# Other order for the second image's direct products around the logits' turns, and a second form for the third image's row at infinity

## The chip, the cores and the metric

The kernel runs on one core of a Trainium2 chip. The metric is the device time of one execution in microseconds (us). Before the change the median of three runs is 669.0 us (668.98, 669.0, 670.58).

The core has five engines that run side by side and wait for each other by semaphores: PE (matrix products; PEld is its loading of weights), DVE (elementwise work), ACT (copies, activations), POOL (here mostly issues of transfers and clearing of buffers) and SP (here only issues of transfers). Each works through its own list of instructions in order.

## The reference

Four images of 256 channels and 64x64 pixels. A 7x7 convolution with dilation 2 and a 1x1 convolution give 49 logits per pixel. Their softmax weights the 49 shifted copies of the image (local attention). The result is whitened in groups of 64 channels.

```python
k = lax.conv_general_dilated(x, w1, (1, 1), [(6, 6), (6, 6)], rhs_dilation=(2, 2), ...) + b1
k = lax.conv_general_dilated(k, w2, (1, 1), [(0, 0), (0, 0)], ...) + b2
attn = softmax(k, axis=1)
xp = jnp.pad(x, ((0, 0), (0, 0), (6, 6), (6, 6)))
shifts = jnp.stack([xp[:, :, 2*u:2*u+64, 2*v:2*v+64] for u in range(7) for v in range(7)], axis=1)
x = jnp.einsum('bkchw,bkhw->bchw', shifts, attn)
# then: mean and 64x64 covariance of each group over all pixels, five Newton steps for
# the inverse square root, and its product with the centred x
```

## The kernel before, in words

The weights of both convolutions are folded into one 7x7 convolution from 256 channels to 49 logits. Everything is float32; the trace records two matmuls for each that the kernel names. Pixels are split by the parity of their row: slot tiles (`slot2`, `slot3` for image 1) each hold one parity of an image.

**The convolution** is done by a Winograd-like scheme: rows are evaluated at seven points, columns at seven points, the products are taken point by point, and both directions are interpolated. Points in a row direction are numbered `br`: 1 to 5, 0, and 6, "infinity" (`INF`). For br 1 to 5 there are products with evaluated data (`conv_bank`, PE at L604, in three banks of column points). The columns are then interpolated into `zz[:, br]` (`col_interp`), and the rows into the logits (`row_interp`, in two parts).

For some rows the columns are not evaluated; the products run directly over the seven column taps:
- `direct` (L779) takes 7 taps x 2 channel chunks x 2 parities (x 2 halves of the columns), 56 matmuls for a whole row at infinity of a later image. So it is done for the row at infinity of images 2 and 3 (`direct_inf`).
- `direct_part` (L862) does the same in three products, each over half as many columns: part 2 takes the even taps, part 1 the odd taps, part 3 the sums of two neighbouring taps with sums of two neighbouring columns of x. Part 3 minus the others gives the odd columns (`direct_ends`). `direct_sums` makes the sums, on DVE. So it is done for image 1's row at infinity and for image 1's row 0 (`direct_start`).

Banks of PSUM: two `cv` banks that are taken in turn (`conv_psum`, `conv_bank`), and two `acc` banks, later used for the attention's sums `y`.

**After the logits** of an image come, for each of two column parities, its turn: PE transposes the logits (L1135), DVE takes the maximum, ACT the exponentials with sums, DVE reciprocals, products and four shuffles (`soft`, `softmax`). Then ACT copies the terms into `zt` (L1253), POOL writes them to memory as `sd` (L1272), and SP reads them back in banded form into `band` and `bandz` (L1322, L1334). PE multiplies the transposed image with the bands (L1442, `first_half` and `second_half`) and turns the result back for the covariance (L1514, L1533).

**What sets the order.** Engines run their lists in order. The first image's part is emitted under `strict[0] = True`: each DVE operation made by `add`, `sub` or `madd` then stands behind the one before it. Later work is a list of steps with costs for each image; after each eighth of the image's cost comes a "gap", in which a half block of the attention of the image before is put (`todo`, `half_gaps`). `conv_step(k, i)` emits bank `i` of row `k` and then prepares the same bank of the next row at once, or, if a gap with a half block follows and the next row is a row 0 at its first bank (`half_next`), behind that gap.

**Around the change**, before: DVE evaluates the first bank of image 1's row 1 (`prepare(NR0, 0)`), then makes the sums for image 1's row at infinity (`direct_sums` into `gbr`, two adds of 512 columns and three of 98), then adds the second half of row 5 of image 0 to `zz` and goes through the second part of `row_interp(0, 1)`, which ends image 0's logits. PE does parts 2 and 1 of the row at infinity into `acc`, then part 3 into a `cv` bank. Then image 0's turn (`soft(0, 0)`), `direct_start(0)` (sums; parts 2 and 1 of row 0 into the two `cv` banks), `direct_start(1)` (part 3 into `acc[0]`), the other turn (`soft(0, 1)`), and the first `conv_step`.

Of the kernel before, what the change touches and what calls it, by code (L numbers as in the profile page):

```python
# [23 lines left out]
INF = 6  # L24
# [8 lines left out]
def kernel(  # L33
# [772 lines left out]
    def direct_sums(b, br, w, room):  # L806

        a = 3 if br == INF else 0
        xs = []
        for h in range(2):  # L810
            x = slots[2 * b + h].rearrange("p c r w -> p (c r w)").rearrange(
                "p (e a w) -> p a e w", a=4, w=SW
            )
            x = x[:, a].rearrange("p e (m i two) -> p i e m two", i=2, two=2)
            o = room[:, h * NX // 2 : (h + 1) * NX // 2]
            add(o.rearrange("p (e m two) -> p e m two", m=SW // 4, two=2), x[:, 0], x[:, 1])
            xs.append(
                o.rearrange("p (c g q w) -> p c g q w", c=NCC, g=2, q=Q8).rearrange(
                    "p c g q (m two) -> p c g q m two", two=2
                )  # L820
            )
        ws = []
        for s, t in enumerate(w):
            nw = (KS // 2) * NCC * KT
            o = room[:, NX + s * nw : NX + (s + 1) * nw]
            o = o.rearrange("p (v a k) -> p v a k", v=KS // 2, a=NCC)
            for j in range(KS // 2):
                add(o[:, j], t[2 * j + 1], t[2 * j])
            ws.append([o[:, j] for j in range(KS // 2)] + [t[KS - 1]])
        return xs, ws  # L830

    def direct_part(b, br, part, ps, w, xs=None):
# [10 lines left out]
        first = True  # L843
        for wt, d in order:
# [51 lines left out]

    def direct_inf(b):

        nc.sync.dma_start(spare[:, :NTAP], kept[INF])
        t = spare[:, :NTAP].rearrange("p (v a k) -> p v a k", v=KS, a=NCC)  # L900
        direct(b, INF, 0, conv_psum(), [t[:, v] for v in range(KS)])

    start_of = {}

    def direct_start(sr):

        n = Q8 + 1
        w = [[gr0[:, v, :, s] for s in range(2)] for v in range(KS)]
        if sr == 0:
            room = store[4].rearrange("p c r w -> p (c r w)")[:, SH * W :]  # L910
            xs, ws = direct_sums(1, 0, [[t[s] for t in w] for s in range(2)], room)
            start_of["xs"] = xs
            start_of["ws"] = [[t[j] for t in ws] for j in range(KS // 2 + 1)]
            p2 = direct_view(conv_psum(), n, M16 + 1)
            direct_part(1, 0, 2, p2, w)
            p1 = direct_view(conv_psum(), n, M16)
            direct_part(1, 0, 1, p1, w)
            direct_ends(0, n, p1, p2)
        else:
            p3 = direct_view(acc[0], n, M16)  # L920
# [3 lines left out]
    acc = [ps_y.tile([P, Q8, W], F32, tag="y", name=f"acc{sr}") for sr in range(2)]  # L924
    for a in acc:
        nc.vector.memset(a, 0.0)
# [14 lines left out]
    def conv_step(k, i):  # L941
# [13 lines left out]
        if k + 1 < len(rows):  # L955
            if half_next[0] and (i, rows[k + 1][1]) == (0, 0):
                after_gap.append(lambda: prepare(k + 1, i, points.append))
            else:
                with tc.high_priority() if last else nullcontext():
                    prepare(k + 1, i, points.append)  # L960
        if i == len(BANKS) - 1 and not end:
# [115 lines left out]
    w = [tap[:, UPOS[3], v] for v in range(KS)]  # L1077
    xs, ws = direct_sums(1, INF, [w], gbr.rearrange("p v a s k -> p (v a s k)"))
    direct0(5, 1)
    row_interp(0, 1)  # L1080

    w = [[t] for t in w]
    p2 = direct_view(acc[0], Q8, M16 + 1)
    direct_part(1, INF, 2, p2, w)
    p1 = direct_view(acc[1], Q8, M16)
    direct_part(1, INF, 1, p1, w)
    p3 = direct_view(conv_psum(), Q8, M16)
    direct_part(1, INF, 3, p3, [[t] for t in ws[0]], xs)
    prepare(NR0, 1)
    prepare(NR0, 2)  # L1090
    strict[0] = False
    direct_ends(INF, Q8, p1, p2)
    direct_ends(INF, Q8, None, None, p3)
# [612 lines left out]
    for b in range(1, B):  # L1706
# [6 lines left out]
        if b == 1:  # L1713
            for sr in range(2):
                steps.insert(sr, (12, lambda sr=sr: direct_start(sr)))
            steps.insert(0, (0, lambda: soft(0, 0)))
            steps.insert(3, (0, lambda: soft(0, 1)))
# [316 lines left out]
```

## Time and profile before

| | |
|---|---|
| median of three runs | 669.0 us |
| the profiled execution | 668.98 us |
| its span, first to last instruction | 667.2 us |
| mean granted PE clock | 0.991 |
| instructions | 19415 |
| DMA packets, bytes | 109840, 126.11 MB |

PE's records by stage of the kernel, from its instructions in order of time:

| stage | us |
|---|---|
| image 0, preparation and its products | 0 to 142.5 |
| image 1, row at infinity in three products | 142.5 to 153.3 |
| first turn of image 0's logits | 154.9 to 156.1 |
| image 1, row 0 in three products | 156.1 to 175.2 |
| image 1's other rows, with image 0's attention between | from 176.8 |
| image 2, row at infinity by `direct` | 273.0 to 284.6 |
| whitening (L1844) | from 613.0 |

How to read it: a line of the time order gives start, length, engine, line of the kernel, operation, output and inputs, size and count; in brackets stands the idle time of that engine before it and what ended it. Matmuls are pipelined, so a record of about 270 ns starts every 55 to 60 ns. "SPq" and "ACTq" are issues of transfers; the data land later. Idle time of an engine that others don't wait for costs nothing.

### The profile page before, as it was taken

What the parts mean: (1) busy time and instruction counts of PE and PEld (TensorE: products, weight loads), DVE (VectorE), ACT (ScalarE), POOL (GpSimd) and SP (SyncE); (2) the same over time, 40 slices, a digit from 0 to 9 for tenths busy, and PEclk for the clock granted to TensorE, in tenths of its full rate; (3) what the DMA queues carried; (4) which work ended last, traced back from release to release, by engine and by line L of the source; (5) the groups of instructions that cost most, each with busy time, mean ns of one, the idle gap of its engine ahead of it and who ended that gap; (6) DMA issues with size and microseconds to landing.
All of it is one profiled execution on the core that took longest, in us unless ns stands there. A gap on an engine that the chain in (4) does not pass through costs nothing.

```text
span 667.2 us, 19415 instructions
## 1 busy us (share of the span) xinstructions
PE 638.7 (96%) x7992; PEld 530.1 (79%) x7992; DVE 571.2 (86%) x1258; ACT 331.8 (50%) x861; POOL 115.3 (17%) x173
## 2 busy tenths in 40 slices
PE   6999999999999999999999999999999999999991
PEld 1439673358999998889999998999999999997440
DVE  3699999999899889999999799989999988634781
ACT  1434331013565566467754554473855667535681
POOL 0000551663213002001022020002220203500000
PEclk9999999999999999999999999999999999999996
DMA  8961799995599988324588673026364325739698
GB/s 316 247 177 67 128 232 382 218 195 83 133 205 223 228 257 304 103 57 108 149 278 278 232 246 107 1 69 195 103 197 112 70 65 129 182 96 380 263 412 335
DMA packets 109840, 126.11 MB, mean 189 GB/s; under 512 B 69127, under 2 KB 92216, under 8 KB 107576
## 3 DMA queue, kind: packets, MB, share of 16 engines
q1 hardware_dynamic: 92952, 69.35, 35.5%
q0 software_dynamic: 10752, 37.26, 21.7%
q10 hardware_dynamic: 6048, 18.27, 8.8%
q8 instruction: 63, 1.03, 0.7%
q14 instruction: 25, 0.20, 0.1%
HBM read 78.78 MB, written 52.36 MB: 197 GB/s over the span
## 4 chain that ended last, share of the span: by engine, by line
PE 62%; DVE 17%; issue 7%; POOL 4%; SPq 4%; DMA 3%; ACT 2%; DVEq 0%; ACTq 0%; POOLq 0%
PE cv L604 25%; PE y L1442 13%; PE sig L1533 5%; PE tp L1514 4%; PE tp L1378 4%; SPq L225 4%; POOL ahead L147 2%; POOL slot L147 2%; PE tp L1844 2%; PE cv L862 2%; DVE zz L352 2%; DVE rb L345 2%; PE cv L779 2%; DVE xh L352 2%; DVE pv L352 1%
## 5 line engine op out<-in xcount | busy, mean ns | idle before, releaser
L604 PE MATMUL cv<-xh,wr 128*49 128x128 f32 x4160 | 232.3, 273 | 0.1
L604 PEld LDWEIGHTS cv<-xh,wr 128*49 128x49 f32 x4160 | 226.2, 124 | 2.9 <-issue 1.0
L1272 POOL DMA_DIRECT2D sd<-zt x120 | 63.3, 534 | 292.2 <-ACT zt L1253 222.2
L1442 PE MATMUL y<-band,xb 128*128 128x209 f32 x448 | 93.7, 341 | 0.6 <-ACT xb L1409 0.6
L1442 PEld LDWEIGHTS y<-band,xb 128*128 128x128 f32 x448 | 75.7, 191 | 1.5 <-ACT xb L1409 0.8
L615 ACT COPY pv<-cv 113x486 f32<-113x486 f32 (+2 forms) x60 | 25.9, 431 | 82.4 <-PE cv L604 82.2
L352 DVE SCALAR_TENSOR_TENSOR pv<-pv 113x162 f32<-113x162 f32 x176 | 52.5, 320 | 1.5 <-ACT pv L615 1.0
L1524 ACT COPY yt<-tp 128x512 f32<-128x512 f32 x60 | 35.0, 591 | 24.3 <-PE tp L1514 23.5
L1253 ACT COPY zt<-d 32x112 f32<-32x112 f32 (+2 forms) x132 | 38.6, 293 | 11.0 <-DVE d L1123 5.1
L1514 PE MATMUL tp<-ident,slot 128*128 128x128 f32 x240 | 41.3, 295 | 0.2 <-ACT slot L1464 0.2
L1378 PE MATMUL tp<-ident,slot 128*128 128x128 f32 x256 | 40.5, 282 | 0.0
L1175 ACT ACTIVATE d<-tp,mx 128x49 f32<-128x49 f32 x96 | 27.4, 321 | 24.2 <-DVE mx L1172 17.6
L1533 PE MATMUL sig<-yt 128*64 128x65 f32 x1024 | 38.0, 225 | 0.9 <-ACT yt L1524 0.9
L1514 PEld LDWEIGHTS tp<-ident,slot 128*128 128x128 f32 x240 | 34.9, 205 | 5.0 <-issue 3.7
L1378 PEld LDWEIGHTS tp<-ident,slot 128*128 128x128 f32 x256 | 38.2, 204 | 0.2 <-issue 0.2
L1533 PEld LDWEIGHTS sig<-yt 128*64 128x64 f32 x1024 | 32.9, 137 | 6.7 <-issue 1.9
L1409 ACT COPY xb<-tp 128x512 f32<-128x512 f32 x52 | 30.6, 588 | 13.7 <-PE tp L1378 10.5
L352 DVE SCALAR_TENSOR_TENSOR xh<-ct 128x512 f32<-128x512 f32 x40 | 26.6, 691 | 5.7 <-PE cv L604 5.4
L147 POOL DMA_DIRECT2D slot<-in_x_dram x12 | 20.4, 1701 | 53.4 <-DVE xh L352 38.6
L348 DVE TENSOR_TENSOR pv<-pv 113x162 f32<-113x162 f32 (+1 forms) x77 | 27.5, 364 | 0.3
L352 DVE SCALAR_TENSOR_TENSOR xh<-xh,rb 128x512 f32<-128x512 f32 x40 | 27.4, 684 | 0.1
L345 DVE TENSOR_TENSOR ct<-rb 128x1024 f32<-128x1024 f32 (+1 forms) x26 | 26.5, 1020 | 0.3
(288 smaller groups left out, 1141.9 us busy)
## 6 DMA issues: line engine op xcount, KB each, us to landing
band<-sd SPq DMA_DIRECT2D x64, 242.0 KB, 3.6
sd<-zt POOLq DMA_DIRECT2D x120, 77.0 KB, 4.2
wr<-gd ACTq DMA_DIRECT2D x14, 588.0 KB, 4.8
wr<-gd ACTq DMA_DIRECT2D x14, 490.0 KB, 4.1
slot<-in_x_dram POOLq DMA_DIRECT2D x12, 512.0 KB, 10.5
ahead<-in_x_dram POOLq DMA_DIRECT2D x12, 512.0 KB, 7.8
spill<-slot POOLq DMA_DIRECT2D x3, 2048.0 KB, 9.4
slot<-ahead POOLq DMA_DIRECT2D x3, 2048.0 KB, 10.7
```

Source lines behind the costliest of these rows:

```text
L147: yield queue.dma_start(o[:, cc, h], src[:, :, pr, h * SW : (h + 1) * SW])
L345: return in_turn(TT(o, a, b, ALU.add))
L352: return in_turn(STT(o, a, f, b, ALU.mult, ALU.add))
L604: nc.tensor.matmul(o, wv[:, sc, sr, cc], xv[bc][:, h * NCC + cc], start=(j == 0), stop=(j == len(terms) - 1), skip_group_check=True,)
L1253: ins = nc.scalar.copy(o, i)
L1272: dma = queue.dma_start(bass.AP(tensor=D.tensor, offset=D.offset + h * HS + g * RS, ap=[[LS, TC], [CR * RS, NCH], [1, KS * WS]],), zt[p0 : ...
L1378: nc.tensor.transpose(t[:, h * C + cc * P : h * C + (cc + 1) * P], tile_of(xt, cc, t8, h, pc), turned_by(n),)
L1409: (nc.vector.tensor_copy if n > 4 * B - 3 else nc.scalar.copy)(xb.rearrange("p a c -> p (a c)"), t[:, : 2 * C])
L1442: nc.tensor.matmul(y_ps[n, half, cc][:, q0 : q0 + nq, c0:c1], xb[:, cc * P : (cc + 1) * P], rhs, start=(k == 0), stop=(k == len(PIECES[hal ...
L1514: nc.tensor.transpose(t[:, h * C + cc * P : h * C + (cc + 1) * P], tile_of(yt, cc, t8, h, pc), turned_by(n),)
L1524: return nc.scalar.copy(yb.rearrange("p h a g c -> p (h a g) c")[:, :, :GW], t[:, : 2 * C].rearrange("p (e c) -> p e c", c=GW),)
L1533: nc.tensor.matmul(sig[g * GW : (g + 1) * GW, cc], yb[:, g, :GW], yb[:, g], start=(count[0] == 0), stop=end, skip_group_check=True,)
```

## The change

Three things, as the code has them:
1. `direct_sums` takes the place for the sums of taps as an argument, and `direct_taps` makes them in one add over all pairs instead of three for each share.
2. Image 1's direct products stand in another order. Parts 2 and 1 of the row at infinity are emitted before `row_interp(0, 1)`, and their ends right behind it; its sums are made between `prepare(NR0, 1)` and `prepare(NR0, 2)`, no longer under the strict order, with x sums in `spare` (the third buffer of `pv`), tap sums in `lgx`, and the last tap copied there by ACT. Its part 3 goes to `third_inf`, into `acc[0]`, in the third step of `direct_start`. `direct_start` now has three steps: sums and the first two taps of part 2; the other two taps and part 1; `third_inf` and part 3, now in `acc[1]`. The turn `soft(0, 0)` stands between the first and the second.
3. `direct_inf` has a second form with three products, whose results are copied out of PSUM by ACT, for an image whose sums `inf_sums` has made ahead. `inf_sums` is called in `conv_step`, in the branch that prepares the next row at once.

```diff
@@ -803,7 +803,7 @@
-    def direct_sums(b, br, w, room):
+    def direct_sums(b, br, w, room, sums):
 
         a = 3 if br == INF else 0
         xs = []
@@ -819,17 +819,17 @@
                     "p c g q (m two) -> p c g q m two", two=2
                 )
             )
-        ws = []
-        for s, t in enumerate(w):
-            nw = (KS // 2) * NCC * KT
-            o = room[:, NX + s * nw : NX + (s + 1) * nw]
-            o = o.rearrange("p (v a k) -> p v a k", v=KS // 2, a=NCC)
-            for j in range(KS // 2):
-                add(o[:, j], t[2 * j + 1], t[2 * j])
-            ws.append([o[:, j] for j in range(KS // 2)] + [t[KS - 1]])
-        return xs, ws
-
-    def direct_part(b, br, part, ps, w, xs=None):
+        return xs, direct_taps(w, sums)
+
+    def direct_taps(w, sums):
+
+        n = w.shape[2]
+        o = sums[:, : KS // 2 * n].rearrange("p (v n) -> p v n", n=n)
+        pair = w[:, : KS - 1].rearrange("p (v two) n -> p two v n", two=2)
+        add(o, pair[:, 1], pair[:, 0])
+        return [o[:, j] for j in range(KS // 2)] + [w[:, KS - 1]]
+
+    def direct_part(b, br, part, ps, w, xs=None, some=slice(None)):
 
         a = 3 if br == INF else 0
         if part == 2:
@@ -840,8 +840,8 @@
             order = [(wj, j - 1) for j, wj in enumerate(w)]
         order.sort(key=lambda p: abs(p[1]))
         lo = -1 if part == 2 else 0
-        first = True
-        for wt, d in order:
+        first = not some.start
+        for wt, d in order[some]:
             for cc in range(NCC):
                 for s in range(len(wt)):
                     for g in range(2):
@@ -894,36 +894,90 @@
+    ahead_inf = {}
+
+    def inf_sums(b):
+
+        nc.sync.dma_start(spare[:, :NTAP], kept[INF])
+        room = rb[1].rearrange("p q r c w -> p (q r c w)")
+        t = spare[:, :NTAP].rearrange("p (v n) -> p v n", v=KS)
+        ahead_inf[b] = direct_sums(b, INF, t, room, room[:, NX:])
+
     def direct_inf(b):
 
+        if b in ahead_inf:
+            xs, ws = ahead_inf[b]
+            t = spare[:, :NTAP].rearrange("p (v a k) -> p v a k", v=KS, a=NCC)
+            one = lambda t: [t.rearrange("p (a k) -> p a k", a=NCC)]
+            w = [[t[:, v]] for v in range(KS)]
+            z = zz[:K2, INF, :Q8].rearrange("p q (m i two) -> p i q m two", i=2, two=2)
+            n2 = Q8 * (M16 + 1) * 2
+            room = rb[1].rearrange("p q r c w -> p (q r c w)")[:K2, 2 * NX - n2 :]
+            copy = direct_view(room.rearrange("p (q w) -> p q w", q=Q8), Q8, M16 + 1)
+            banks = [conv_psum() for _ in range(2)]
+            p3 = direct_view(banks[0], Q8, M16)
+            direct_part(b, INF, 3, p3, [one(t) for t in ws], xs)
+            with tc.high_priority():
+                nc.scalar.copy(z[:, 1], p3[:K2])
+            p2 = direct_view(banks[1], Q8, M16 + 1)
+            direct_part(b, INF, 2, p2, w)
+            with tc.high_priority():
+                nc.scalar.copy(room, p2[:K2].rearrange("p q m two -> p (q m two)"))
+            p1 = direct_view(banks[0], Q8, M16)
+            direct_part(b, INF, 1, p1, w)
+            with tc.high_priority():
+                nc.scalar.copy(z[:, 0], p1[:K2])
+            ncv[0] += 1
+
+            def ends():
+                sub(z[:, 1], z[:, 1], z[:, 0])
+                sub(z[:, 1], z[:, 1], copy[:, :, 1:])
+                add(z[:, 0], z[:, 0], copy[:, :, :M16])
+
+            ends()
+            return
         nc.sync.dma_start(spare[:, :NTAP], kept[INF])
         t = spare[:, :NTAP].rearrange("p (v a k) -> p v a k", v=KS, a=NCC)
         direct(b, INF, 0, conv_psum(), [t[:, v] for v in range(KS)])
 
-    start_of = {}
-
-    def direct_start(sr):
-
-        n = Q8 + 1
-        w = [[gr0[:, v, :, s] for s in range(2)] for v in range(KS)]
-        if sr == 0:
-            room = store[4].rearrange("p c r w -> p (c r w)")[:, SH * W :]
-            xs, ws = direct_sums(1, 0, [[t[s] for t in w] for s in range(2)], room)
-            start_of["xs"] = xs
-            start_of["ws"] = [[t[j] for t in ws] for j in range(KS // 2 + 1)]
-            p2 = direct_view(conv_psum(), n, M16 + 1)
-            direct_part(1, 0, 2, p2, w)
-            p1 = direct_view(conv_psum(), n, M16)
-            direct_part(1, 0, 1, p1, w)
-            direct_ends(0, n, p1, p2)
-        else:
-            p3 = direct_view(acc[0], n, M16)
-            direct_part(1, 0, 3, p3, start_of["ws"], start_of["xs"])
-            direct_ends(0, n, None, None, p3)
-
     acc = [ps_y.tile([P, Q8, W], F32, tag="y", name=f"acc{sr}") for sr in range(2)]
     for a in acc:
         nc.vector.memset(a, 0.0)
+    start_of = {}
+
+    def direct_start(sr):
+
+        n = Q8 + 1
+        if sr == 0:
+            by_share = lambda t: [
+                t.rearrange("p (a s k) -> p a s k", a=NCC, s=2)[:, :, k] for k in range(2)
+            ]
+            g = lgx[:, : KS * 2 * NCC * KT].rearrange("p (v n) -> p v n", v=KS)
+            room = store[4].rearrange("p c r w -> p (c r w)")[:, SH * W :]
+            xs, ws = direct_sums(1, 0, g, room, room[:, NX:])
+            start_of["xs"] = xs
+            start_of["ws"] = [by_share(t) for t in ws]
+            w = [by_share(g[:, v]) for v in range(KS)]
+            p2 = direct_view(conv_psum(), n, M16 + 1)
+            direct_part(1, 0, 2, p2, w, some=slice(0, 2))
+            start_of["w"], start_of["p2"] = w, p2
+        elif sr == 1:
+            direct_part(1, 0, 2, start_of["p2"], start_of["w"], some=slice(2, 4))
+            p1 = direct_view(conv_psum(), n, M16)
+            direct_part(1, 0, 1, p1, start_of["w"])
+            direct_ends(0, n, p1, start_of["p2"])
+        else:
+            third_inf()
+            p3 = direct_view(acc[1], n, M16)
+            direct_part(1, 0, 3, p3, start_of["ws"], start_of["xs"])
+            direct_ends(0, n, None, None, p3)
+
+    def third_inf():
+
+        p3 = direct_view(acc[0], Q8, M16)
+        direct_part(1, INF, 3, p3, start_of["ws_inf"], start_of["xs_inf"])
+        direct_ends(INF, Q8, None, None, p3)
+
     rows = [(0, br) for br in (1, 2, 3)]
     NR0 = len(rows)
     rows += [(b, br) for b in range(1, B) for br in ROWS if b > 1 or br]
@@ -958,6 +1012,8 @@
             else:
                 with tc.high_priority() if last else nullcontext():
                     prepare(k + 1, i, points.append)
+                if end and i == 0 and b == 1:
+                    inf_sums(b + 1)
         if i == len(BANKS) - 1 and not end:
             with in_order() if last else nullcontext():
                 col_interp(b, br)
@@ -1074,23 +1130,24 @@
     col_interp(0, 3)
     row_interp(0, 0)
     prepare(NR0, 0)
-    w = [tap[:, UPOS[3], v] for v in range(KS)]
-    xs, ws = direct_sums(1, INF, [w], gbr.rearrange("p v a s k -> p (v a s k)"))
     direct0(5, 1)
+    g = tap[:, UPOS[3]].rearrange("p v a k -> p v (a k)")
+    one = lambda t: [t.rearrange("p (a k) -> p a k", a=NCC)]
+    p2 = direct_view(acc[0], Q8, M16 + 1)
+    direct_part(1, INF, 2, p2, [one(g[:, v]) for v in range(KS)])
+    p1 = direct_view(acc[1], Q8, M16)
+    direct_part(1, INF, 1, p1, [one(g[:, v]) for v in range(KS)])
     row_interp(0, 1)
-
-    w = [[t] for t in w]
-    p2 = direct_view(acc[0], Q8, M16 + 1)
-    direct_part(1, INF, 2, p2, w)
-    p1 = direct_view(acc[1], Q8, M16)
-    direct_part(1, INF, 1, p1, w)
-    p3 = direct_view(conv_psum(), Q8, M16)
-    direct_part(1, INF, 3, p3, [[t] for t in ws[0]], xs)
+    direct_ends(INF, Q8, p1, p2)
     prepare(NR0, 1)
+    strict[0] = False
+    room = lgx[:, 2 * KS * NCC * KT :]
+    start_of["xs_inf"], ws = direct_sums(1, INF, g, spare, room)
+    start_of["ws_inf"] = [one(t) for t in ws]
     prepare(NR0, 2)
-    strict[0] = False
-    direct_ends(INF, Q8, p1, p2)
-    direct_ends(INF, Q8, None, None, p3)
+    last_tap = room[:, KS // 2 * NCC * KT :][:, : NCC * KT]
+    nc.scalar.copy(last_tap, g[:, KS - 1])
+    start_of["ws_inf"][-1] = one(last_tap)
     gpool.release()
 
 
@@ -1711,10 +1768,13 @@
                 for i, cost in enumerate((6, 5, 2)):
                     steps.append((cost, lambda k=k, i=i: conv_step(k, i)))
         if b == 1:
-            for sr in range(2):
-                steps.insert(sr, (12, lambda sr=sr: direct_start(sr)))
-            steps.insert(0, (0, lambda: soft(0, 0)))
-            steps.insert(3, (0, lambda: soft(0, 1)))
+            steps[:0] = [
+                (0, lambda: direct_start(0)),
+                (0, lambda: soft(0, 0)),
+                (12, lambda: direct_start(1)),
+                (12, lambda: direct_start(2)),
+                (0, lambda: soft(0, 1)),
+            ]
         else:
             steps.insert(0, (12, lambda b=b: direct_inf(b)))
         j, at, whole = 0, 0, sum(c for c, _ in steps)
```

More of the change, by code (lines that the diff above doesn't have):

```diff
@@ L901, in direct_inf @@
         direct(b, INF, 0, conv_psum(), [t[:, v] for v in range(KS)])
+    acc = [ps_y.tile([P, Q8, W], F32, tag="y", name=f"acc{sr}") for sr in range(2)]
+    for a in acc:
+        nc.vector.memset(a, 0.0)
     start_of = {}
@@ L907, in direct_start @@
         n = Q8 + 1
-        w = [[gr0[:, v, :, s] for s in range(2)] for v in range(KS)]
         if sr == 0:
+            by_share = lambda t: [
+                t.rearrange("p (a s k) -> p a s k", a=NCC, s=2)[:, :, k] for k in range(2)
+            ]
+            g = lgx[:, : KS * 2 * NCC * KT].rearrange("p (v n) -> p v n", v=KS)
             room = store[4].rearrange("p c r w -> p (c r w)")[:, SH * W :]
-            xs, ws = direct_sums(1, 0, [[t[s] for t in w] for s in range(2)], room)
+            xs, ws = direct_sums(1, 0, g, room, room[:, NX:])
             start_of["xs"] = xs
-            start_of["ws"] = [[t[j] for t in ws] for j in range(KS // 2 + 1)]
+            start_of["ws"] = [by_share(t) for t in ws]
+            w = [by_share(g[:, v]) for v in range(KS)]
             p2 = direct_view(conv_psum(), n, M16 + 1)
-            direct_part(1, 0, 2, p2, w)
+            direct_part(1, 0, 2, p2, w, some=slice(0, 2))
+            start_of["w"], start_of["p2"] = w, p2
+        elif sr == 1:
+            direct_part(1, 0, 2, start_of["p2"], start_of["w"], some=slice(2, 4))
             p1 = direct_view(conv_psum(), n, M16)
-            direct_part(1, 0, 1, p1, w)
-            direct_ends(0, n, p1, p2)
-        else:
-            p3 = direct_view(acc[0], n, M16)
+            direct_part(1, 0, 1, p1, start_of["w"])
+            direct_ends(0, n, p1, start_of["p2"])
+        else:
+            third_inf()
+            p3 = direct_view(acc[1], n, M16)
             direct_part(1, 0, 3, p3, start_of["ws"], start_of["xs"])
             direct_ends(0, n, None, None, p3)
-    acc = [ps_y.tile([P, Q8, W], F32, tag="y", name=f"acc{sr}") for sr in range(2)]
-    for a in acc:
-        nc.vector.memset(a, 0.0)
+    def third_inf():
+        p3 = direct_view(acc[0], Q8, M16)
+        direct_part(1, INF, 3, p3, start_of["ws_inf"], start_of["xs_inf"])
+        direct_ends(INF, Q8, None, None, p3)
     rows = [(0, br) for br in (1, 2, 3)]
```

## The prediction

> **What bounds the kernel now.** I read the page's busy times first, then busy time by stretch, then PE's and DVE's instructions in order of time where the change lies (142 to 177 us), then the DMAs behind them.
>
> ```profile
> PE 638.7 (96%) x7992; PEld 530.1 (79%) x7992; DVE 571.2 (86%) x1258; ACT 331.8 (50%) x861; POOL 115.3 (17%) x173
> ```
>
> The busy time by stretch (busy us and count for PE, PEld, DVE, ACT, POOL; then clock, DMA share, GB/s):
>
> ```profile
> 142.50:156.10 13.60, 11.01 (x188) 10.42 (x184) 13.33 (x19) 3.34 (x6) 9.47 (x8) 1.00 0.98 161
> 156.10:176.83 20.73, 20.73 (x366) 20.44 (x365) 20.50 (x43) 8.85 (x45) 5.07 (x10) 1.00 0.36 62
> 176.83:273.00 96.17, 94.72 (x1409) 91.70 (x1409) 86.91 (x202) 59.09 (x158) 13.77 (x26) 1.00 0.93 235
> ```
>
> PE is full from 156 us on; up to 600 us it has some 3 us of gaps. In the first stretch it idles 2.6 of 13.6 us while DVE is busy. PE in order of time (start, length, instructions, idle before it and what ended that):
>
> ```profile
> 142.50 6.36 PE L862 MATMUL acc<-slot,tap 128*49 128x128 f32 x112
> 149.80 2.72 PE L862 MATMUL cv<-gbr 128*49 128x128 f32 x48 [0.94 <-DVE gbr L345]
> 154.94 1.21 PE L1135 MATMUL tp<-ident,slot 113*128 113x113 f32 x8 [1.65 <-ACT slot L746]
> 156.08 12.63 PE L862 MATMUL cv<-slot,lgx 128*49 128x128 f32 x224
> 168.54 5.19 PE L862 MATMUL acc<-slot 128*49 128x128 f32 x96
> 176.83 9.81 PE L604 MATMUL cv<-xh,wr 128*49 128x128 f32 x176
> 186.57 0.98 PE L1442 MATMUL y<-band,xb 128*128 128x209 f32 x4
> ```
>
> Two waits, 0.94 + 1.65 = 2.59 us. The first is for the sums of image 2's row at infinity; the second for the logits, whose DVE chain stands behind the same sums. DVE in that time:
>
> ```profile
> 148.02 1.29 DVE L345 TENSOR_TENSOR gbr<-slot 128x512 f32<-128x512 f32 x2
> 149.23 0.59 DVE L345 TENSOR_TENSOR gbr<-tap 128x98 f32<-128x98 f32 x3
> 149.74 0.61 DVE L345 TENSOR_TENSOR zz<-zz,cv 113x448 f32<-113x448 f32 x1
> 153.44 0.69 DVE L352 SCALAR_TENSOR_TENSOR slot<-zz 113x512 f32<-113x512 f32 x1
> 166.47 0.85 DVE L345 TENSOR_TENSOR slot<-lgx 128x98 f32<-128x98 f32 x4
> 167.24 2.28 DVE L348 TENSOR_TENSOR rb<-rb,rb 128x2048 f32<-128x2048 f32 x1
> 176.45 1.05 DVE L1171 TENSOR_REDUCE mx<-tp 128x8 f32<-128x392 f32 x2 [0.16 <-PE tp L1135]
> 178.83 0.69 DVE L345 TENSOR_TENSOR xh<-ct 128x512 f32<-128x512 f32 x1 [1.12 <-PE cv L604]
> 180.58 0.69 DVE L348 TENSOR_TENSOR xh<-ct 128x512 f32<-128x512 f32 x1 [1.05 <-PE cv L604]
> ```
>
> DVE has no gap from 138.57 to 176.29 us; after that it waits for PE.
>
> **The change, part by part.** I followed it in the order of the changed program's instructions on each engine.
>
> *Sums out of the logits' way.* The five adds at 148.02 to 149.74 go behind the logits' chain, so the chain starts 1.72 us sooner: ACT's bias (154.16 before) at 152.44, PE's eight transposes at 153.22.
>
> *Product order on PE.* The count is unchanged (224 + 128 + 112 + 64 at L862). After the two products that end at 148.86 PE no longer waits: the first half of part 2 of row 0 follows, 64 records at 55.7 ns (12.46 us / 224), to 152.42. Idle until 153.22: 0.80 us, one gap for two. Then transposes 1.14 (154.94 to 156.08) to 154.36; 160 records 8.91 to 163.27; the 64 of infinity's third part 3.49 (149.80 to 153.29) to 166.76; 128 of row 0's third part 6.66 to 173.42; transposes of blocks and logits 1.63 to 175.05. The L604 run starts there, not at 176.83: 2.59 - 0.80 = **1.79 us sooner**.
>
> *Does DVE deliver?* It has to by PE's times: infinity's sums (now after the maxima) end about 158.3, needed 163.27; row 0's end about 162.2, needed 166.76. So both are hidden, with 4.5 us or more to spare; without that cover PE would wait their 1.7 and 2 us.
>
> *Wider adds.* Nine adds of 98 columns become one of 294 and one of 588. The nine step by 0.51 + 0.17 + 0.18 + 0.77 = 1.63 us. No row shows the new widths. The 294 lies between the 98-wide (0.17) and the 392-wide (0.49: d<-d,rm, 162.16 to 162.65), the 588 between the 512-wide (0.62) and the 1024-wide (1.14): saved -0.00 to 0.84. On the line from 0.18 at 98 to 0.62 at 512 they cost 0.39 + 0.70, nearest to the 392 and 512 rows: 0.54 saved. DVE's list then ends at 175.75, not 176.29. That alone moves no PE time; it keeps DVE ahead of PE, which gives DVE the logits at about 174.5 and frees xh at 177.04, so DVE meets L604 with 1.79 regained by its waits (1.12 + 1.05, and another 1.05 at 193.53).
>
> *What gets late.* The first softmax's reciprocals now stand behind those sums and the 2.2 us subtraction of rb. Adding DVE's steps from 148.02: sums done 162.2, subtraction 164.4, reciprocals, masks and products 165.9, one add of zz 166.3, four shuffles to 169.4 (166.73 before). Behind the shuffles wait, on ACT, eleven copies (3.33 us), then POOL's eight writes of sd, then SP's loads of the bands, and behind these on SP the loads of a slot. All go 2.6 us later:
>
> ```profile
> 176.94 0.91 SPq L1322 DMA_DIRECT2D band<-sd  x2
> 177.90 2.59 SPq L1334 DMA_DIRECT2D bandz<-sd  x4
> ```
>
> The first band took 3.6 us to land, 180.5; now 183.2. PE reaches its band product at 186.57 - 1.79 = 184.78. Hidden, with 1.6 us of cover left of 6.
>
> *One more copy* (128x98, ACT) stands behind the last copy of lgx, which ends at 95.01; ACT then idles 0.45 us for PE. A 144-wide copy takes 0.33, so the gap hides it; uncovered it would cost at most that.
>
> *The third image.* The sums that would open its three products hang on the branch taken when the next row is prepared at once. At that step (row 5, first bank: (76 + 6) x 8 = 656 >= 7 x 89 = 623, in a listed gap) the other branch is taken. The changed order still has the direct products (56 matmuls, 112 records, and one 113x512 copy). No term for this part.
>
> **The sum.** The profiled execution took 668.98 us (span 667.2 and 1.8 around it), the median of three is 669.0. After 176.83 PE is nearly full in all stretches up to 600 us and its few waits are for work that PE itself set off, so the 1.79 carries: 669.0 - 1.8 = **667.2 us**.
>
> **Rivals.**
> *DVE sets the pace.* In 142.5 to 156.1 DVE is the full engine. If the stretch behind it also runs at DVE's pace, only the work taken off DVE counts: 0.5 us, 668.5. Against it: DVE's waits of 1.12 and 1.05 us for L604 right after. [...]
>
> *The bands land late* (the other side). The second pair of bands, issued from 180.5 with the weights' load out from 182.38, took 7.5 us to land, not 3.6. If the first pair, now issued at 179.55 with those weights at about 181.7, takes 7.5 as well, it lands at 187.05 and PE starts its band product 0.5 later than before: 669.5. It decides from a landing after 186.6 on; 671 would need 9 us. For it: the overlap is new; against it: most of the first pair is in before the weights move. [...]
>
> *Both gaps go*: if DVE's chain gains 0.8 more (no dependent steps next to each other), 2.59 us: 666.4.
>
> *The third image's part runs after all*: 112 records in 11.65 us become 176 at 55.7 ns, 9.8: another 1.8, 665.4. The order speaks against it.
>
> **How the numbers follow.** Forecast 0.58, DVE's pace 0.12, late bands 0.13, both gaps 0.15, third image 0.02. What can be told from no change is about 0.3%, 2.0 us: below 667.0 or above 671.0. The forecast lies 0.2 from that line, so half of it counts as faster: 0.29 + 0.15 + 0.02 = 0.46. Slower: 0.08 of the late bands'. Within: the rest, 0.29 + 0.12 + 0.05 = 0.46. The range runs from both gaps and 0.4 of DVE's saving, 666.0, to the late bands, 669.6; the likeliest case's own is 666.6 to 667.8.
>
> **What would show it.** Right: no wait of L862 for DVE; about 0.8 us before the logits' transposes; the first L604 run at 175.0 and the first band product at 184.8, neither waiting for a DMA; shuffles ending near 169.4; bands issued near 179.5; the third image still with 112 records of direct products. Wrong: DVE idle for PE before 176 us, a band product that waits for a landing, or a shift at 177 us that is gone by 273 us.

## The result, and the profile after

The changed kernel takes 667.42 us (median of six, 666.99 to 667.99); the kernel before took 669.75 us beside it (668.98 to 670.75). The ratio is 0.9966 with a 95% interval of 0.9953 to 0.9978: faster by 0.22 to 0.47%. The profiled executions took 667.38 us (span 665.6) and 668.98 us (span 667.2), 1.6 us apart. The medians lie 2.3 us apart because the times of the kernel before fall into two groups, about 669.0 and 670.6; three of these six are in the upper one. In three later comparisons its median was 669.02, 669.2 and 669.02 (31, 20 and 14 executions), which puts the change at 1.6 to 1.8 us. What such an upper group is, the last experiment shows for the kernel with the wide adds.

The busy times of the changed kernel on its page, and its busy time by stretch (PE, PEld, DVE, ACT, POOL; then clock, DMA share, GB/s):

```profile
PE 638.4 (96%) x7992; PEld 529.9 (80%) x7992; DVE 570.9 (86%) x1251; ACT 331.7 (50%) x862; POOL 115.0 (17%) x173
```

```profile
142.50:156.10 13.60, 12.81 (x218) 12.45 (x216) 13.29 (x18) 3.23 (x6) 5.42 (x4) 1.00 1.04 162
176.83:273.00 96.17, 94.08 (x1388) 90.68 (x1386) 87.52 (x204) 59.58 (x159) 13.73 (x26) 1.00 0.96 237
```

PE does the same 7992 matmuls. In the first stretch it idles 0.8 us where it idled 2.6, but behind 176.83 it idles 2.1 us where it idled 1.4. So something was gained at the change and a part of it was lost again later. PE of the changed kernel in order of time shows both (start, length, instructions, idle before it and what ended that; the code's lines behind L862 have moved, L1135 is now L1192, L1442 is L1499):

```profile
142.39 6.36 PE L862 MATMUL acc<-slot,tap 128*49 128x128 f32 x112
148.59 3.75 PE L862 MATMUL cv<-slot,lgx 128*49 128x128 f32 x64
153.13 1.21 PE L1192 MATMUL tp<-ident,slot 113*128 113x113 f32 x8 [0.79 <-ACT slot L746]
154.27 9.04 PE L862 MATMUL cv<-slot,lgx 128*49 128x128 f32 x160
163.15 3.45 PE L862 MATMUL acc<-pv,lgx 128*49 128x128 f32 x64
...
174.71 9.82 PE L604 MATMUL cv<-xh,wr 128*49 128x128 f32 x176
185.16 0.95 PE L1499 MATMUL y<-band,xb 128*128 128x209 f32 x4 [0.64 <-DMA band<-sd]
```

One gap of 0.79 us stands where two of 0.94 and 1.65 stood. From the first L862 record to the first L604 run it takes 32.32 us, where it took 34.33: 2.0 us sooner. Then there is a wait that the kernel before did not have: the first band product waits 0.64 us for its band. DVE of the changed kernel:

```profile
147.93 0.61 DVE L345 TENSOR_TENSOR zz<-zz,cv 113x448 f32<-113x448 f32 x1
157.78 0.46 DVE L345 TENSOR_TENSOR lgx<-tap 128x294 f32<-128x294 f32 x1
161.17 0.76 DVE L345 TENSOR_TENSOR slot<-lgx 128x588 f32<-128x588 f32 x1
161.85 2.28 DVE L348 TENSOR_TENSOR rb<-rb,rb 128x2048 f32<-128x2048 f32 x1
168.02 0.95 DVE L1180 STREAM_SHUFFLE d<-d 128x224 f32<-128x224 f32 x1
```

The logits' chain starts at 147.93, not 149.74; the wide adds stand behind the maxima and the 2.28 us subtraction still stands ahead of the shuffles, whose last one ends at 168.97 (166.73 before). Behind these come the bands. All engines' records of the changed kernel at that time, cut to the bands and to the weights that ACT loads, and the landing of the bands as the view of their tile gives it:

```profile
180.10 0.90 SPq L1379 DMA_DIRECT2D band<-sd  x2
180.21 0.34 ACTq L417 DMA_DIRECT2D wr<-gd  x1
...
DMA to landing us min/median/max: 4.9/5.2/5.8
```

The bands are issued 3.2 us later than before (176.94), and the weights' load 2.2 us sooner (182.38): both now start at the same time. The first band load landed at 185.03, 4.92 us after its issue, and PE started at 185.16; before, the first took 3.61. A part of the bands' delay arose ahead of them: they are issued when the seventh of POOL's eight writes of `sd` has landed, and that write took 5.08 us (175.01 to 180.09), where it took 4.15 before (172.78 to 176.92).

Compared at the same instructions, PE is 1.43 us ahead of the kernel before at 208 us and 1.51 us ahead at 558 us. The third image's row at infinity is still 112 records of `direct` in 11.66 us.

### The profile page after: what moved, and what is told of

It reads as the page before. It is cut to its first block, busy times and chain, and to the rows that moved or that the text cites. A ratio compares the mean times of both kernels' runs of the same rounds, so it can differ in the third digit from the quotient of the medians.

```text
span 665.6 us, 19407 instructions
## 1 busy us (share of the span) xinstructions
PE 638.4 (96%) x7992; PEld 529.9 (80%) x7992; DVE 570.9 (86%) x1251; ACT 331.7 (50%) x862; POOL 115.0 (17%) x173
## 4 chain that ended last, share of the span: by engine, by line
PE 74%; DVE 16%; issue 3%; DMA 2%; ACT 2%; POOL 1%; DVEq 0%; SPq 0%; ACTq 0%; POOLq 0%
PE cv L604 29%; PE y L1499 13%; PE acc L779 7%; PE sig L1590 5%; PE tp L1571 4%; PE tp L1435 4%; PE cv L779 3%; PE cv L251 2%; DVE zz L352 2%; PE tp L1904 2%; DVE ct L352 2%; DVE pv L352 2%; DVE zz L348 2%; DVE zz L345 1%; PE cv L1904 1%
## 5 line engine op out<-in xcount | busy, mean ns | idle before, releaser
L604 PE MATMUL cv<-xh,wr 128*49 128x128 f32 x4160 | 232.3, 273 | 0.1
L604 PEld LDWEIGHTS cv<-xh,wr 128*49 128x49 f32 x4160 | 226.2, 124 | 3.0 <-issue 1.0
L1499 PE MATMUL y<-band,xb 128*128 128x209 f32 x448 | 93.6, 341 | 1.2 <-DMA band<-sd 0.6
L1499 PEld LDWEIGHTS y<-band,xb 128*128 128x128 f32 x448 | 75.7, 191 | 2.1 <-ACT pv L615 0.9
L352 DVE SCALAR_TENSOR_TENSOR rb<-slot 128x1024 f32<-128x1024 f32 (+1 forms) x26 | 26.9, 1065 | 0.0
```

Of the source, the lines that this page charges most:

```text
L352: return in_turn(STT(o, a, f, b, ALU.mult, ALU.add))
L604: nc.tensor.matmul(o, wv[:, sc, sr, cc], xv[bc][:, h * NCC + cc], start=(j == 0), stop=(j == len(terms) - 1), skip_group_check=True,)
L1499: nc.tensor.matmul(y_ps[n, half, cc][:, q0 : q0 + nq, c0:c1], xb[:, cc * P : (cc + 1) * P], rhs, start=(k == 0), stop=(k == len(PIECES[hal ...
```

## The experiments

All times in us. "Gap" is PE's idle time ahead of the first logits' transposes, "stage" the time from the first L862 record to image 1's first L604 run, "band" PE's wait for the first band; ratios are to the kernel before on the same chip. The span and the three columns behind it are of the one execution that was profiled. Line numbers differ by a few between the versions.

| kernel | median | ratio (95%) | span | gap | stage | band |
|---|---|---|---|---|---|---|
| before | 669.75 | 1 | 667.2 | 0.94 + 1.65 | 34.33 | 0 |
| after | 667.42 | 0.9966 (0.9953 to 0.9978) | 665.6 | 0.79 | 32.32 | 0.64 |
| e1_wide_only | 669.55 | 1.0006 (0.9995 to 1.0018) | 666.7 | 0.95 + 1.48 | 34.17 | 0 |
| e2_narrow | 668.08 | 0.9982 (0.9972 to 0.9991) | 667.1 | 0.78 | 32.30 | 0.83 |
| e3_sums_first | 670.26 | 1.0021 (1.0001 to 1.0041) | 668.3 | 2.34 | 35.49 | 0 |
| e4_late | 669.69 | 1.0006 (0.9994 to 1.0018) | 667.8 | 0.8 | 32.30 | 2.10 |
| e5_bands_first | 667.94 | 0.9972 (0.9962 to 0.9982) | 665.9 | 0.8 | 32.31 | 0 |
| e6_three_taps | 666.37 | 0.9947 (0.9934 to 0.996) | 664.2 | 0 | 31.45 | 0 |
| e7_both | 666.39 | 0.997 (0.9951 to 0.999) | 664.5 | 0 | 31.46 | 0 |
| e8_third_on | 679.25 | 1.0139 (1.0124 to 1.0154) | 677.9 | 0.8 | 32.32 | 0.56 |
| e9_third_early | 667.91 | 0.9978 (0.9968 to 0.9987) | 667.7 | 0.8 | 32.29 | 0.73 |
| e10_taps_third | 666.37 | 0.9962 (0.9949 to 0.9975) | 664.5 | 0 | 31.47 | 0 |
| e11_again | 667.3 (one) | | 665.4 | 0.8 | 32.29 | 0.47 |
| e12_wide_again | 670.48 (one) | | 668.6 | 0.99 + 1.48 | 35.79 | 0 |

**e1_wide_only and e2_narrow: the width of the adds.** The first puts the wide adds alone into the kernel before, the second takes them out of the changed one. The edit of e2:

```diff
-        add(o, pair[:, 1], pair[:, 0])
+        m = NCC * KT
+        for j in range(KS // 2):
+            for c in range(0, n, m):
+                add(o[:, j, c : c + m], pair[:, 1, j, c : c + m], pair[:, 0, j, c : c + m])
```

> The kernel before with the wider adds alone (one of 294 and one of 588 columns for nine of 98). My theory (PE gains by the order, not by DVE's work): the first logits' transposes start at most 0.15 us sooner (154.8 for 154.94), the first L604 run at 176.7 for 176.83, time within 0.2 us of before. Rival (DVE sets the pace): the 0.5 us taken off DVE show at 177 us and in the time, 0.5 us less than before.

> The changed kernel with the nine narrow adds back (three and six of 98 columns) in the new order. My theory: L604 still starts near 174.7 us and PE's gap before the transposes stays 0.8; only the terms get later by 0.5, so the wait for the first band grows from 0.64 to about 1.1, and the time is 0.5 us above the changed kernel's, still 1.2 us or more below before. Rival (DVE sets the pace): L604 itself starts 0.5 us later, at 175.2.

Alone, the wide adds shorten the gap by 0.17 and the stage by 0.16; the median does not tell them from nothing. Without them the changed kernel's stage is as long as with them (32.30 and 32.32): the products' order and the place of the sums make the whole of the 2.0. Its median is 0.7 above the changed kernel's, and its profile (of the slowest of ten executions) shows losses elsewhere: the shuffles end 0.65 later (0.2 of that arose ahead of 142 us), the band wait is 0.83, and a second band product, at 562 us, waits 0.61 where the changed kernel does not wait.

**e3_sums_first: the place of the sums.** The changed kernel, with the sums for the row at infinity put back ahead of the logits' chain:

```diff
+    room = lgx[:, 2 * KS * NCC * KT :]
+    start_of["xs_inf"], ws = direct_sums(1, INF, g, spare, room)
+    start_of["ws_inf"] = [one(t) for t in ws]
     direct0(5, 1)
...
     prepare(NR0, 1)
     strict[0] = False
-    room = lgx[:, 2 * KS * NCC * KT :]
-    start_of["xs_inf"], ws = direct_sums(1, INF, g, spare, room)
-    start_of["ws_inf"] = [one(t) for t in ws]
```

> The changed kernel with the sums for the second image's row at infinity put back in front of the logits' chain; the order of products on PE stays the new one. My theory: the logits' chain is late again, PE idles about 2.4 us before the transposes (start near 154.7), L604 starts at 176.3 and the time is within 0.5 us of before. Rival (the order of products on PE is what gains): PE idles no more than 1 us and the time stays within 0.5 us of the changed kernel's.

PE of this kernel in order of time, and its busy time and clock by stretch:

```profile
154.81 1.22 PE L1192 MATMUL tp<-ident,slot 113*128 113x113 f32 x8 [2.34 <-ACT slot L746]
155.96 10.65 PE L862 MATMUL cv<-slot,lgx 128*49 128x128 f32 x160
178.00 2.17 PE L604 MATMUL cv<-xh,wr 128*49 128x128 f32 x36
```

```profile
156.00:160.00 4.00, 4.00 (x45) 4.00 (x46) 4.00 (x10) 2.96 (x22) 0.00 (x0) 0.57 0.28 42
160.00:166.50 6.50, 6.50 (x123) 6.50 (x120) 6.50 (x12) 1.67 (x12) 0.00 (x0) 1.00 0.01 4
```

The stage is 3.17 longer than the changed kernel's. Of that, 1.55 is the longer gap (2.34 against 0.79), which is the DVE time of the three adds (148.03 to 149.61, 1.58). The rest is in the 160 records behind the gap: 10.65 us, where they took 9.04, since the granted clock was 0.57 from 156 to 160. Without the move of the sums the other order of the products is no faster than the kernel before: seven of ten executions took 670.15 us or more at a mean granted clock of 0.988 to 0.990 (two of them 672.65 and 675.32, not explained), and the three at 0.991 or 0.992 took 668.57 to 669.25, about as long as the lower group of the kernel before. I had seen only the gap in it, not the clock behind it. The reverse, the sums moved and the old order of the products kept, was not run.

**e4_late and e5_bands_first: the cover of the bands.** The first puts two idle operations (a maximum of `d` with itself) ahead of the first shuffles. The second holds the rb subtraction and two operations of row 3's evaluation behind the shuffles (the edit of e5, cut to the subtraction):

```diff
         elif br == 2:
-            sub(r[0], r[0], r[1])
+            with tc.issue_after(turned[3].ins) if b == 1 else nullcontext():
+                sub(r[0], r[0], r[1])
```

> The changed kernel with two adds' worth of work in front of the first shuffles (the maximum of the terms with themselves, 784 columns, which alters no value). It makes the terms of the first turn about 3.2 us later and touches nothing on PE up to the first band product. If the landing of the first bands is the wait that now ends last: PE's wait before the first band product grows from 0.64 to about 3.9 us and the time by about 3.2 us, to 670.6. Rival (the 0.64 us are made up for later): the wait grows, but the time by less than 1 us.

> The changed kernel with the subtraction and the evaluation of rb for the next rows held until the first turn's shuffles are issued; nothing is taken out. The shuffles then end about 1.8 us sooner (167.1 for 168.97), the bands are issued near 178.3 and land before PE comes at 184.5. My theory (the bands are the last wait there): no wait before the first band product, time 0.6 us below the changed kernel's. Rival (DVE sets the pace up to 177 us, or what is held is late for the next L604 run): L604 or the run after it starts later and nothing is gained.

PE of e4:

```profile
186.50 0.95 PE L1503 MATMUL y<-band,xb 128*128 128x209 f32 x4 [2.10 <-DMA band<-sd]
```

In e4 the shuffles end 3.15 later (172.1), but the bands are issued only 1.4 later (181.51), and PE waits 2.10 for the first, 1.46 longer: each microsecond by which the bands are late is paid, since no cover is left. So the expected 3.9 was not reached. The median is 2.3 above the changed kernel's; beside the 1.46, PE loses 0.3 at 288 us (waiting for ACT's copy of `xb`) and 0.5 around a band at 563 us. In e5 the shuffles end at 167.6, the bands are issued at 179.12 and the wait is gone: PE is 2.16 us ahead of the kernel before at 208 us, where the changed kernel is 1.43 ahead. Yet the time is no better. PE waits 0.85 instead of 0.57 for ACT's copy of `xb` at 286 us, and loses another 0.5 around a band at 562 us (0.33 ahead of the changed kernel at 561.11, 0.20 behind it at 564.48):

```profile
561.11 0.87 PE L1503 MATMUL y<-band,xbs 128*128 128x209 f32 x4
562.24 2.39 PE L1503 MATMUL y<-band,xbs 128*128 128x209 f32 x12 [0.26 <-DMA band<-sd]
```

The first four products run; those behind them need the second band of the pair. In the changed kernel that was issued at 557.79 and landed 4.06 later, at 561.85, before PE came to it; here, issued at 557.65, it took 4.55 and landed at 562.20. So the bands have some 4 us there in each version, about as long as they take to land (4.90 in e2), and which version waits is settled by tenths.

**e6_three_taps and e7_both: the remaining gap.** e6 puts three of part 2's four taps ahead of the logits' transposes instead of two; e7 is e6 with e5.

```diff
-            direct_part(1, 0, 2, p2, w, some=slice(0, 2))
+            direct_part(1, 0, 2, p2, w, some=slice(0, 3))
...
-            direct_part(1, 0, 2, start_of["p2"], start_of["w"], some=slice(2, 4))
+            direct_part(1, 0, 2, start_of["p2"], start_of["w"], some=slice(3, 4))
```

> The changed kernel with three of the four taps of part 2 ahead of the first transposes, not two: 96 records, so that PE has no gap before the transposes. L604 starts 0.8 us sooner, at 173.9. My theory: the bands land when they did, so PE's wait before the first band product grows from 0.64 to 1.4 us and the time stays within 0.2 us of the changed kernel's. Rival (the gap before the transposes is still what ends last): the time falls by 0.8 us.

> The two edits of the runs before together: bands first, and three taps ahead of the transposes. My theory: both gaps go, 0.64 + 0.79 = 1.4 us below the changed kernel's time, L604 at 173.9, first band product at 183.7 without a wait. Rival: DVE, which then has 1.4 us less to catch up, makes PE wait at the next run for evaluated data, and the gain stays at 0.6 us.

PE of e6 in order of time:

```profile
148.68 5.55 PE L862 MATMUL cv<-slot,lgx 128*49 128x128 f32 x96
154.16 1.21 PE L1192 MATMUL tp<-ident,slot 113*128 113x113 f32 x8
173.94 9.81 PE L604 MATMUL cv<-xh,wr 128*49 128x128 f32 x176
183.68 0.98 PE L1499 MATMUL y<-band,xb 128*128 128x209 f32 x4
```

Its bands and weights, and the landing of the bands:

```profile
179.54 0.90 SPq L1379 DMA_DIRECT2D band<-sd  x2
180.42 0.33 ACTq L417 DMA_DIRECT2D wr<-gd  x1
...
DMA to landing us min/median/max: 2.8/3.1/3.3
```

The gap is gone and the stage is 0.87 shorter, although the transposes come 1.0 later. My theory, that the later turn would make the bands later by as much, was wrong: POOL's writes began 0.5 later (172.36), but the bands were issued at 179.54, 0.56 sooner than in the changed kernel, landed in 2.8 to 3.3 us, and PE did not wait. The writes were done sooner since the seventh took 4.00 us, not 5.08. What differs beside it is SP's 686 KB load of `lgx`, issued at 172.43, with the first write, where the changed kernel issued it at 173.20, among them; that this is why is not shown. The gain of 0.87 + 0.64 carries: at 208 us and at 558 us PE is 1.4 us ahead of the changed kernel, and the profiled times differ by 1.3, the medians by 1.05. This version, 666.06 to 666.66 us in five executions, beats both kernels (the changed one took 666.99 to 667.99). In e7, e5's edit adds nothing to it; three of its twelve times lie at 671.1 to 671.7, with a mean granted clock of 0.987 where the others have 0.991 to 0.993; where in the kernel it fell was not profiled.

**What decides the landing.** The first two band loads (242 KB each) and the first load of weights (ACT, 588 KB) in every version; "lead" is how far the bands were issued ahead of the weights, "lgx ahead" how far SP's load of `lgx` (686 KB) had been issued ahead of the bands, "landing" the time from issue to landing of the first and the second band load:

| kernel | bands issued | weights issued | lead | lgx ahead | landing |
|---|---|---|---|---|---|
| before | 176.94 | 182.38 | 5.44 | 1.6 | 3.6, 3.7 |
| e12 | 178.87 | 184.01 | 5.14 | 1.9 | 4.2, 4.3 |
| e3 | 179.06 | 183.51 | 4.45 | 2.6 | 3.9, 3.9 |
| e7 | 179.54 | 182.91 | 3.37 | 6.9 | 2.8, 2.9 |
| e1 | 180.04 | 182.10 | 2.06 | 5.0 | 3.4, 3.5 |
| e5 | 179.12 | 181.14 | 2.02 | 6.0 | 3.5, 3.5 |
| e10 | 179.45 | 180.42 | 0.97 | 7.0 | 2.7, 3.2 |
| e6 | 179.54 | 180.42 | 0.88 | 7.1 | 2.8, 3.1 |
| after | 180.10 | 180.21 | 0.11 | 6.9 | 4.9, 5.2 |
| e4 | 181.51 | 181.53 | 0.02 | 8.4 | 4.9, 5.2 |
| e9 | 180.51 | 180.44 | -0.07 | 7.1 | 4.8, 5.1 |
| e11 | 180.43 | 180.32 | -0.11 | 7.1 | 4.5, 4.9 |
| e8 | 180.73 | 180.44 | -0.29 | 7.3 | 4.4, 4.8 |
| e2 | 181.13 | 180.55 | -0.58 | 7.8 | 4.3, 4.6 |

With a lead over the weights of 0.11 us or less they land in 4.3 to 5.2 us. With a lead of 0.9 us or more they land in 2.7 to 3.5 us where the load of `lgx` was issued 5 us or more ahead, and in 3.6 to 4.3 us where it was issued 1.6 to 2.6 us ahead. So the lead over the weights is not all of it: e12, with a lead of 5.1, lands about as late as e2. That other loads under way make the bands land late is my reading of these fourteen profiles: no run moved the load of weights or that of `lgx` alone, so it rests on this table.

> The changed kernel once more, unchanged, to see what of its profile repeats. If the 5.0 us landing of the first band follows from the kernel's order of transfers, PE waits 0.6 us for it again at 185 us. If it varies from execution to execution, the landing is somewhere between the 2.8 and 5.4 us of the other versions and the wait is another one, or none.

The unchanged kernel waited again, 0.47 us (the first band landed at 184.97 and PE started at 185.11). The record names ACT's copy of `pv` from 184.68 to 185.11 here, as in e8 and e9; but in the kernel before, in e5 and in e6 the first band product starts 0.1 us ahead of that copy, so it does not need it. The wait came back with this order of transfers, in both executions of the changed kernel that were profiled.

**e8_third_on, e9_third_early, e10_taps_third: the third image's three products.** In e8 the sums are made in the branch that is taken, behind the gap's work. In e9 they are made ahead of it, and part 3, which needs them, comes last; e10 is e9 with e6. The edit of e9, cut (the banks of the parts change with their order; in e8 the call stands behind `prepare` in the work put behind the gap):

```diff
+                if end and b == 1:
+                    inf_sums(b + 1)
                 after_gap.append(lambda: prepare(k + 1, i, points.append))
...
-            direct_part(b, INF, 3, p3, [one(t) for t in ws], xs)
...
             direct_part(b, INF, 2, p2, w)
...
             direct_part(b, INF, 1, p1, w)
...
+            direct_part(b, INF, 3, p3, [one(t) for t in ws], xs)
```

> The changed kernel with the third image's sums made also in the branch that prepares the next row behind the gap, so that its row at infinity runs in three products as the code means. PE: 112 records in 11.65 us become 176 at 55.7 ns, 9.8 us: 1.8 us less. DVE: two adds of 512 columns (0.61 each), one of 294 (0.37) and three of 256 for the ends (0.33 each), 2.6 us more, in a stretch where DVE has no gap between 247 and 290 us. Theory A (PE sets the pace there): 1.8 us below the changed kernel's time. Theory B (DVE does): PE waits for DVE between 285 and 310 us, and the time is at best the same, up to 0.9 us above.

> The changed kernel, with image 2's row at infinity really in three products, its sums made ahead of the gap (among image 1's last column interpolation, DVE position 402 to 408 of 1020) and its products in the order part 2, part 1, part 3, so that the sums have 112 records, some 6.4 us, of cover. Theory (only the place of the sums cost 12.2 us in e8): PE waits for no sum, the row takes 176 records at 55.7 ns, 9.8 us, in place of 11.66, and the time is 667.4 - 1.8 = 665.6. Rival (DVE is the full engine there, 26.93 of 27 us between 273 and 300): the sums (1.6 us by 0.69 + 0.69 + 0.46 less overlap) and two more operations of some 0.42 us come out of DVE's list behind which the next rows stand, and PE gets them back as waits behind the row: 667.4 to 668.

> The same together with three taps of part 2 ahead of the logits' transposes. If the two gains add: 666.4 - 1.8 = 664.6. If DVE takes the third image's part back: 666.4 to 667.

PE of e8, where the row starts with part 3:

```profile
284.12 4.41 PE L862 MATMUL cv<-rb 128*49 128x128 f32 x48 [12.22 <-DVE rb L345]
```

DVE made the sums one by one among the interpolation of image 1's last rows, the last of them at 283.61 to 283.99, and PE stood for 12.22 us (its 48 records then took 4.41 us, not 2.69, at a clock of 0.55). Against the changed kernel it cost 11.8 us. With the sums early and part 3 last, PE of e9:

```profile
271.88 6.36 PE L862 MATMUL cv<-slot,pv 128*49 128x128 f32 x112
278.07 2.69 PE L862 MATMUL cv<-rb 128*49 128x128 f32 x48
280.58 0.94 PE L862 MATMUL cv<-rb,pv 128*49 128x96 f32 x16
...
347.78 7.11 PE L604 MATMUL cv<-xh,wr 128*49 128x128 f32 x96 [2.07 <-DVE xh L345]
```

The row takes 9.6 us instead of 11.6, as counted. Then PE waits 0.41 us for a band at 321 us (0.69 in e10) and 2.07 us for DVE at 347 us (1.82 in e10), waits that the changed kernel does not have, and the gain is gone. This execution, 669.49 us, was the slowest of ten (666.95 to 668.21 the others); in it the clock fell behind the second wait (96 records in 7.11 us, 5.45 in e10). In e10, where it did not, PE gains 2.4 us on the changed kernel by 300 us and loses 0.95 around the band and 2.0 at the wait for DVE. Busy time in that stretch, first the changed kernel, then e9:

```profile
273.00:348.00 75.00, 74.43 (x1034) 69.71 (x1032) 74.93 (x158) 46.21 (x155) 6.86 (x13) 1.00 0.46 140
```

```profile
273.00:348.00 75.00, 72.41 (x1076) 69.47 (x1074) 74.78 (x164) 46.28 (x154) 6.85 (x13) 1.00 0.47 141
```

DVE is full for 75 us in both; PE happens to be full as well. The three products take 2.0 us off PE and put six more records on DVE, so PE only waits longer. By the medians nothing is won: 667.91 against 667.42, and with three taps 666.37 against 666.37.

**e12_wide_again: the two groups of times.** Ten times of e1 lay in two groups, 668.46 to 668.86 and 670.23 to 670.89; its profile was of the lower.

> The kernel before with the wide adds, once more, unchanged. Its ten times lie in two groups, 668.46 to 668.86 and 670.23 to 670.89, and the profiled one (668.46) shows full clock behind the gap of 1.48 us ahead of the logits' transposes. If this execution is of the upper group, theory: the granted clock falls behind that gap, and the 160 to 224 records of L862 behind it take some 1.6 us longer, as behind the 2.34 us gap of e3_sums_first (10.65 in place of 9.04). Rival: the 1.6 us lie elsewhere (at the start or in the whitening), and the clock behind the gap is 1.00. If it is of the lower group, the clock is 1.00 there and nothing is learnt of the upper one.

This execution took 670.48 us. Its PE, and clock by stretch:

```profile
155.04 1.21 PE L1142 MATMUL tp<-ident,slot 113*128 113x113 f32 x8 [1.48 <-ACT slot L746]
156.18 14.21 PE L862 MATMUL cv<-slot,lgx 128*49 128x128 f32 x224
```

```profile
156.00:160.00 4.00, 4.00 (x43) 3.81 (x43) 3.93 (x10) 2.66 (x19) 1.23 (x4) 0.57 0.66 96
160.00:167.00 7.00, 7.00 (x132) 7.00 (x128) 6.99 (x17) 1.98 (x14) 0.00 (x0) 1.00 0.02 4
```

In the first execution of this kernel the 224 records took 12.63 us behind the same gap of 1.48, at a clock of 1.00; here they took 14.21, at 0.57 for about 4 us. That is 1.58 of the 1.9 us between the two spans; another 0.3 arose ahead of 142 us. The kernel before has the same place with a gap of 1.65 and the same two groups (in the comparison with e1, 26 times from 668.72 to 669.69 and 5 from 670.44 to 670.80); that its upper group is the same fall of the clock in the same place was not profiled. But the mean granted clock of each execution in the comparisons with the experiments is on record: the 16 executions of the kernel before at 670.38 us or more have 0.989 or 0.990, the 50 others 0.991 to 0.993. A fall to 0.57 for 4 us of 667 lowers the mean by 0.0026 (an estimate from e12's figures), so it fits. The changed kernel's gap is 0.79. Its six executions, e11's one and those of e2, e5 and e6, 31 together, all have 0.991 or more. So the loss of 1.6 us, which met a quarter of the executions of the kernel before, has not shown in the mean clock with the shorter gap or none, but for e7's three. The mean is no sharp mark: the profiled execution of e9, in which the clock fell behind the second wait, has 0.991.

## Why the prediction was right, and where not

**The order of the products: right.** The gap came out at 0.79 (0.80 foretold), the transposes at 153.13 (153.22). L604 started at 174.71, not 175.05: 0.11 of that had arisen ahead of the change, and the 64 records of the row's third part took 3.28 from start to next start where the sum had 3.49. So the term of 1.79 measured 2.0. (The first of the two waits is for the sums of image 1, the second image; the prediction says image 2.)

**DVE as the pace: fell.** The wide adds alone shorten the stage by 0.16 (e1), and taking them out does not lengthen it (e2). The 0.54 us of DVE's work were priced well (the adds stepped by 0.37 and 0.68, where 0.39 and 0.70 were estimated), and are worth next to nothing in PE's time up to 177 us, as the prediction said; what e2 lost, 0.7 in the median, came by the bands as far as its profile shows.

**Sums hidden behind PE: right.** L862 waits for no DVE operation. e3 shows the price if they are not moved: 1.55 us of gap, and 1.6 more of clock, which no step of the prediction had.

**What gets late: the step that failed.** The prediction kept 1.6 us of cover: bands issued at 179.5, landed 3.6 later, needed at 184.78. The shuffles ended at 168.97, even sooner than the 169.4 foretold. But the prediction kept the 10.2 us from there to the bands as they were, and they took 11.1, since POOL's writes landed later: the bands were issued at 180.10. It moved the weights' load by 0.7, to about 181.7, and it came 2.2 sooner, as PE did, at 180.21, right with the bands. And it kept the landing at 3.6 us, which was 4.9. The wait was 0.64. This is the mechanism of the rival "the bands land late", which knew only a landing of 7.5 us and let it decide from 186.6 on, though by its own times PE needed the band at 184.78. That the bands are the wait is shown by e4, e5 and e11; that the weights make them land late is argued from the table above.

**Third image: right that it did not run, wrong in its price.** The branch was not taken. Had it been, the "another 1.8" would have been 11.8 us lost as written (e8), and with the sums in time nothing at all (e9, e10), since DVE is full from 273 to 348 us and a band came late at 320 us.

**The sum.** 2.0 gained, 0.64 given back, 1.4 to 1.5 carried to 558 us, 1.6 in the profiled times. The mechanism of the gain was the one foretold. That the forecast of 1.8 came so close is luck in part: one term was 0.2 too small, and another, 0.64, was missing. "Both gaps go" did not come by itself. In e6 both are gone (a stage shorter by 2.88, where the rival had 2.59) and the band wait with them: 666.37 against the rival's 666.4. It came not by a shorter chain on DVE, as that rival had it, but by one more tap of PE's own work ahead of the transposes.

## What to carry to other kernels

Fill a wait of the full engine with work whose inputs are ready, and move work of another engine out of the chain that ends the wait: here that gave 2.0 us with not one instruction less on PE, while 0.5 us off the busiest engine of the stretch gave 0.2 at most. Then look at what the earlier start brings together: a transfer that was issued 5.4 us ahead of another one may now be issued with it, and its cover must be counted with a landing time measured in that order (4.9 us here, not 3.6). Work taken off PE in a stretch where DVE is full as well can turn up as a wait for DVE some 70 us later (e9, e10), so look for it far behind the change.

## What the runs showed of the hardware

**The clock behind short waits.** PE waits of 1.48 (e12), 2.34 (e3) and 2.07 us (e9, where the 96 records behind it took 7.11 us and 5.45 in e10) were each followed by about 4 us at a granted clock of 0.57 to 0.59, which cost 1.6 to 1.7 us each time. The same waits in other executions and others of like length (1.48 in e1, 1.65 before, 1.82 in e10, 2.10 in e4) were followed by a clock of 1.00. A mean clock of 0.990 or less, as such a fall would give by the estimate made with e12, is on record for 5 of 10 executions of e1, 16 of 66 of the kernel before, 7 of 10 of e3 and 2 of 10 of e4; where the clock fell in those that were not profiled is not shown. So neither the length of the wait nor its place decides it alone (1.48 us at the same place in e1 and e12, with a clock of 1.00 and of 0.57 behind it); what does is not shown.

**Landing times.** The same 242 KB load of a band (the first two of each profile) took from 2.7 to 5.2 us: 4.3 to 5.2 where a 588 KB load was issued within 0.6 us of it, otherwise 3.6 to 4.3 where one of 686 KB had been issued 1.6 to 2.6 us ahead, and 2.7 to 3.5 where that one was 5 us or more ahead. Why is not shown by a run that moves one load alone.
